# Helping a depthwise convolution: one multiplication and one adding transfer per tap, on wide tiles, and more taps

## The chip, the cores and the metric

The kernel runs on one core of one Trainium2 chip. The metric is the device time of one execution in microseconds (us). The core's engines appear as PE (TensorE, matmuls), PEld (its weight loads), DVE (VectorE), ACT (ScalarE), POOL (GpSimd) and SP (SyncE). GpSimd and SyncE issue the DMA transfers that matter here: GpSimd's go through queue q0, SyncE's through q1, and both are served by the same 16 DMA engines.

## The reference

Eight images of 384 channels and 32 x 32 places, all in f32, pass through two blocks:

```python
# block 0: attention and MLP, over the 1024 places of an image as tokens
h = layernorm(t, g1, beta1)                        # over the 384 channels
q, k, v = split(h @ w_qkv.T + b_qkv)               # 8 heads of 48
t = t + (softmax(q @ k.T * 48**-0.5) @ v) @ w_proj.T + b_proj
h = layernorm(t, g2, beta2)
t = t + gelu_tanh(h @ w_fc1.T + b_fc1) @ w_fc2.T + b_fc2     # 1536 hidden
# block 1: depthwise convolution, MLP with a global response normalization
y = depthwise_conv_7x7(x, dw_w, padding=3) + dw_b  # each channel by its own 49 taps
y = layernorm(y, ln_w, ln_b)
y = gelu(y @ w1 + b1)                              # 1536 hidden
nx = norm_over_places(y) / (mean_over_channels(norm_over_places(y)) + 1e-6)
x = x + (grn_gamma * (y * nx) + grn_beta + y) @ w2 + b2
```

## The kernel before

**Layout.** An image lies in SBUF with its channels on partitions: 3 channel tiles (`ct`, 0 to 2) of 128 partitions by N = 1024 places. `half(h)` is one of the two halves of 512 places. `pad` holds the same image with a border of three places for the convolution, and `acc` the sums of the convolution, [128, 3, 1024]. A matmul of TensorE takes 128 x 512 places at a time.

**Order of the work.** Block 1 of image b-1 runs between the parts of block 0 of image b. One image b (the loop is `for b in range(B)` near the end of the kernel) goes through these stages: the products for q and k (`qk`); attention (64 steps, one head and one block of 128 keys in each: scores at L818, exponential at L827, product with v two steps later at L838); the MLP (`mlp`); the first product of block 1 of image b-1 (`grn_up`); v of the next image (`values`, from `next_values`); the second product of block 1 (`grn_down`), for which y is scaled at L1473. Most products are done by fast schemes with fewer products (15 for 3 x 3 by 2 x 2 blocks) whose operands are sums of blocks; L480 is the evacuation of such a sum or product on ScalarE, L496 and L467 are matmuls of it.

**The flow.** The order of the instructions on each engine is fixed when the program is built. TensorE's main path is written out; with each matmul, `flow.pe(us)` moves a virtual time on (`U` = 0.857 us for 128 x 512). Everything else is a chain (a Python generator) that yields the time it wants to wait; when the virtual time has passed it, the chain records its next instructions. A `paced` chain counts from the time it was due.

**The convolution.** A tap is one of the 49 weights of the 7 x 7 window. VectorE takes most taps: `convolution` (L1244), one instruction a tap and channel tile, `acc = window * weight + acc`. The rest are the helped taps. `help_convolution` takes the last `HELPED[ct]` taps of the list `TAPS` for each channel tile, tile 2 first, then 1, then 0: ScalarE multiplies a window of `pad` by the weight into a tile `tap` (L1279), and GpSimd issues a DMA transfer that adds this tile to `acc` (L1280). A helped tap is done in two halves of 512 places, one instruction and one transfer of 256 KB each, 2.5 us of virtual time apart. The last eight taps of the list are, in order, 48, 23, 3, 10, 17, 31, 38, 45; so HELPED = 5, 7, 7 helps 10 to 45 of channel tile 0 and 23 to 45 of tiles 1 and 2.

`start_conv` spawns both chains for image b behind `grn_up` of image b-1; they run on beside v, the second product of block 1, and q, k and attention of the next image. `taken[ct]` keeps VectorE off the channel tile that is being helped, until 8 us of virtual time after its last helped tap. While the list `quiet` has an entry (during `grn_down`), the helper waits. Images 0 to 6 have helped taps; image 7's convolution runs otherwise.

**Tiles named "res".** The products of helped taps lie in tiles of the tag "res": four buffers of [128, 512] in the pool `three`. A tile that takes a buffer again waits until the last use of this buffer is done, here until the transfer of four halves ago has landed. Three other places use the tag: the loads of the residual in the last product (`grn_down_straight`), a spare of the preparation in image 0 (`spare`), and the four tiles of the first layernorm of the next image (`places` in `norm_of_next`).

**Layernorm.** It sums squares over the 384 channels: VectorE adds the three channel tiles (`ln_sq`), and TensorE sums over partitions with a matmul by ones. `token_sums` first folds `ln_sq`, with `fold="columns"` by two DMA transfers of GpSimd that add one half of the partitions to the other (L526), and then sums with matmuls (L532, `ln_var`) over 64 partitions. The second layernorm of block 0 does this in the second half of attention, where its chain stands beside the helped taps.

Of the kernel before, what the change touches and what calls it, by code (L numbers as in the profile page):

```python
# [46 lines left out]
F32 = mybir.dt.float32  # L47
AF = mybir.ActivationFunctionType
ALU = mybir.AluOpType
AX = mybir.AxisListType  # L50

P = 128
B, C, H, W = 8, 384, 32, 32
N = H * W
# [5 lines left out]
KS, PAD = 7, 3  # L60
HP, WP = H + 2 * PAD, W + 2 * PAD
NH = N // 2
# [2 lines left out]
CM = 2  # L65
NC = HT // CM
U = 0.857
HELPED = 5, 7, 7
BEGUN = 5
SCALE = HD ** -0.5  # L70
EPS0, EPS1, GRN_EPS = 1e-5, 1e-6, 1e-6
# [105 lines left out]
def block_kernel(  # L177
# [16 lines left out]
    nc = tc.nc  # L194
# [4 lines left out]
    two = ctx.enter_context(tc.tile_pool(name="two", bufs=2))  # L199
# [30 lines left out]
    def half(h):  # L230
        return slice(h * NH, (h + 1) * NH)
# [36 lines left out]
    def col(name, i):  # L268
        at, width = VEC[name]
        assert i < width  # L270
        return vec[:, at + i : at + i + 1]
# [4 lines left out]
    def image(ap):  # L276
        return ap.rearrange("p (h w) -> p h w", w=W)

    def o_tile(name):
        return ps_o.tile([P, NH], F32, tag="o", name=name)  # L280

    def s_tile(name):
        return ps_s.tile([P, N], F32, tag="s", name=name)
# [979 lines left out]
    def help_convolution(acc, us, taken):  # L1263

        yield 8.0
        for ct in reversed(range(CT)):
            taken[ct] = float("inf")
            for i in TAPS[KS * KS - HELPED[ct] :]:
                dy, dx = divmod(i, KS)
                for h in range(2):  # L1270
                    if quiet:
                        while quiet:
                            yield 1.0
                        yield 3.0
                    t = three.tile([P, NH], F32, tag="res", bufs=4, name=f"tap_{ct}_{i}_{h}")
                    y0 = dy + h * H // 2
                    window = pad[:, ct, y0 : y0 + H // 2, dx : dx + W]
                    tap = col("dww", ct * KS * KS + i)
                    nc.scalar.mul(t.rearrange("p (h w) -> p h w", w=W), window, tap)  # L1279
                    nc.gpsimd.dma_start(out=acc[:, ct, half(h)], in_=t, accum_op=ALU.add)  # L1280
                    yield us
            taken[ct] = flow.now + 8.0
        yield 8.0
        taken.clear()
# [73 lines left out]
    def grn_down_straight(b, y, kept, weights, tag, index, todo):  # L1358


        rows = [r for r, _ in todo]
        res = []

        def load():
            if len(res) < len(todo):
                r, part = todo[len(res)]
                t = three.tile([P, NH], F32, tag="res", bufs=4, name=f"res_{b}_{r}_{part.start}")[:, : part.stop - part.start]
                nc.sync.dma_start(out=t, in_=kept[r * P : (r + 1) * P, part])
                res.append(t)

        for _ in range(3):
            load()
        for n, (r, part) in enumerate(todo):
            keys = RAW[2 * r : 2 * r + 2]
            tiles = [weights.at(f"w2_{tag}", key)[:, k, :] for key in keys for k in range(HT // 2)]
            ps = o_tile(f"o2_{b}_{r}")[:, : part.stop - part.start]
            for k in range(HT):
                nc.tensor.matmul(out=ps, lhsT=tiles[k], rhs=y(k, part), start=(k == 0), stop=(k == HT - 1))  # L1378
                flow.pe(U * (part.stop - part.start) / NH)
                if k == 2 and rows.index(r) == n and r + 1 in rows:  # L1380
                    for key in RAW[2 * r + 2 : 2 * r + 4]:
                        scaled(b, weights.at(f"w2_{tag}", key), key, True)
            if r not in rows[n + 1 :]:
                for key in keys:
                    weights.used(f"w2_{tag}", key)
            nc.vector.scalar_tensor_tensor(res[n], ps, b2[:, r : r + 1], res[n], ALU.add, ALU.add)
            nc.sync.dma_start(out=image_of(out, index)[r * P : (r + 1) * P, part], in_=res[n])
            load()
# [253 lines left out]
    def prepare(weights, aside):  # L1642
# [19 lines left out]
            return parts  # L1662

        def spare(name):
            return three.tile([P, NH], F32, tag="res", bufs=4, name=name)

        def forms(name, w, store):
            def keep_form(i, t):
# [198 lines left out]
    def main():  # L1867
# [55 lines left out]
        def start_conv(b, us, *first):  # L1923
            acc = state["acc"] = one.tile([P, CT, N], F32, tag="acc", name=f"acc_{b}")
            taken = {}
            state["conv"] = flow.spawn(convolution(acc, us, first, taken=taken, helped=HELPED, begun=state.pop("begun", {})), paced=True)
            state["help"] = flow.spawn(help_convolution(acc, 2.5, taken), paced=True)

        def conv_norm(b, ln):

# [44 lines left out]
        def norm_of_next(b, us):  # L1975

            xn, name = state["xn"], f"ln1_{b + 1}"
            gates["ln1"] = 0
            places = [three.tile([P, NH], F32, tag="res", bufs=4, name=f"{name}_{i}") for i in range(4)]
            pairs = [(h, places[2 * h], places[2 * h + 1]) for h in range(2)]  # L1980
            quarters = [slice(j * NH // 2, (j + 1) * NH // 2) for j in range(2)]

            def fold(t, h):
                nc.gpsimd.dma_start(out=t[ROWS[h], :], in_=t[ROWS[1 - h], :], accum_op=ALU.add)

            def strip(h, j):
                return slice(64 * h + 32 * j, 64 * h + 32 * j + 32)

            def fold_again(t, h):
                for j, q in enumerate(quarters):  # L1990
                    nc.gpsimd.dma_start(out=t[strip(h, j), q], in_=t[strip(h, 1 - j), q], accum_op=ALU.add)

            def totals(kind, of):

                both_banks = s_tile(f"{name}_{kind}0").rearrange("p (j n) -> p j n", j=2)[:, :, : NH // 2]
                single = [o_tile(f"{name}_{kind}1_{j}")[:, : NH // 2] for j in range(2)]
                for h in range(2):
                    for j, q in enumerate(quarters):
                        out = single[j] if h else both_banks[:, j, :]
                        rows = strip(h, j)  # L2000
                        nc.tensor.matmul(out=out, lhsT=ones[rows, :], rhs=of[h][rows, q], start=True, stop=True)
                flow.pe(U / 2)
                whole = lambda t: t.rearrange("p (j n) -> p j n", j=2)
                return [[(both_banks, whole)], [(single[j], lambda t, q=q: t[:, q]) for j, q in enumerate(quarters)]]

            for h, a, _ in pairs:
                nc.vector.tensor_tensor(a, xn[:, 0, half(h)], xn[:, 1, half(h)], ALU.add)
            for h, a, _ in pairs:
                nc.vector.tensor_tensor(a, a, xn[:, 2, half(h)], ALU.add)
                fold(a, h)  # L2010
            yield 8.0
            for h, a, _ in pairs:
                fold_again(a, h)
            yield us - 8.0
            sums = totals("sum", [a for _, a, _ in pairs])
            yield 0.8
            for h, a, square in pairs:
                for ct in range(CT):
                    part = xn[:, ct, half(h)]
                    for ps, view in sums[h]:  # L2020
                        nc.vector.scalar_tensor_tensor(view(part), ps, -1.0 / C, view(part), ALU.mult, ALU.add)
                    if ct < 2:
                        nc.scalar.activation((square, a)[ct], part, AF.Square)
                yield 3.0
            for h, a, square in pairs:
                nc.vector.tensor_tensor(square, square, a, ALU.add)
                nc.scalar.activation(a, xn[:, 2, half(h)], AF.Square)
                yield 1.5
            for h, a, square in pairs:
                nc.vector.tensor_tensor(square, square, a, ALU.add)  # L2030
                fold(square, h)
            yield 5.0
            for h, _, square in pairs:
                fold_again(square, h)
            yield 8.0
            sums = totals("var", [square for _, _, square in pairs])
            yield 0.8
            ln_table()
            for h, a, _ in pairs:
                for ps, view in sums[h]:  # L2040
                    nc.scalar.activation(view(a), ps, AF.Ln, bias=eps0, scale=1.0 / C)
                nc.scalar.activation(a, a, AF.Exp, scale=-0.5)
            for h, a, _ in pairs:
                for ct in range(CT):
                    yield from gated("ln1")
                    part = xn[:, ct, half(h)]
                    nc.vector.scalar_tensor_tensor(part, part, col("g1", ct), a, ALU.mult, ALU.mult)
# [257 lines left out]
```

## Time and profile before

| | |
|---|---|
| time, median of 3 runs | 3212.09 us (3211.55 to 3214.67) |
| profiled execution, its own time | 3213.02 us |
| its span | 3211.1 us, 39348 instructions |
| mean granted clock of TensorE | 0.999 |
| PE busy | 3196.2 us (100%), 14204 matmuls |
| DVE busy | 2550.4 us (79%), 3587 instructions |
| ACT busy | 1674.6 us (52%), 2363 instructions |
| POOL busy | 493.4 us (15%), 592 instructions |
| DMA | 393.09 MB, mean 122 GB/s; q0 26.6% and q1 23.6% of the 16 engines' span |
| L1244, DVE, taps of the convolution, 815 of one group of shapes | 911.0 us, 1157 ns each |
| L827, ACT, exponentials 128x1024, 512 | 524.3 us, 1025 ns each |
| L1279, ACT, helped taps 128x512, 266 | 195.1 us, 736 ns each |
| L1280, POOL, issues of adding transfers, 266 | 227.0 us, 859 ns each |
| adding transfers acc<-tap, 256.0 KB | 3.5 us median from issue to landing |

Busy times are those of one profiled execution; matmuls are pipelined and their ends are modelled, so a busy PE can still have waited. A row of the page names line, engine, operation and the tiles out<-in, then the count, the busy time and the mean of one, then the idle time of the engine just before these instructions and what ended most of it. An arrow such as "<-DMA acc<-tap" names what released the instruction.

### The profile page before, as it was taken

To read this page: it belongs to the slowest core of one execution; us is meant where nothing else is said; L and a number is where in the kernel's file an instruction comes from. 1 tells how busy PE (TensorE), PEld (TensorE's weight loads), DVE (VectorE), ACT (ScalarE), POOL (GpSimd) and SP (SyncE) were. 2 spreads that over 40 slices of the span, in tenths; PEclk is the share of its full clock that TensorE was granted. 3 is DMA by queue.
4 is the path that set the end of the run, shared out by engine and by line. 5 is a ranking of instruction groups with operands and counts; after the bars stand their busy time and mean duration, and the time that the engine had idled before them with its cause. 6 is when DMAs were issued, how large, how long until landed. Compare 5 with 4: busy or idle time off the path is not lost.

```text
span 3211.1 us, 39348 instructions
## 1 busy us (share of the span) xinstructions
PE 3196.2 (100%) x14204; PEld 1402.1 (44%) x14204; DVE 2550.4 (79%) x3587; ACT 1674.6 (52%) x2363; POOL 493.4 (15%) x592
## 2 busy tenths in 40 slices
PE   9999999999999999999999999999999999999999
PEld 5344434443444434444344443444435444344454
DVE  4547788897878978789787888888887788879964
ACT  3542763456644476444754637637365374732543
POOL 2102211112111121201112011120111201200000
PEclk9999999999999999999999999999999999999999
DMA  6435742647346564456546374463743638433244
GB/s 210 155 127 170 168 90 50 162 112 165 84 88 159 123 151 92 97 142 158 115 92 124 116 186 97 81 136 106 194 92 80 148 97 200 72 81 93 55 119 111
DMA packets 206052, 393.09 MB, mean 122 GB/s; under 512 B 42656, under 2 KB 48416, under 8 KB 205472
## 3 DMA queue, kind: packets, MB, share of 16 engines
q0 software_dynamic: 79296, 163.35, 26.6%
q1 hardware_dynamic: 126272, 226.49, 23.6%
q8 instruction: 114, 1.87, 0.2%
q10 hardware_dynamic: 288, 0.71, 0.1%
q14 instruction: 82, 0.67, 0.1%
HBM read 212.98 MB, written 40.11 MB: 79 GB/s over the span
## 4 chain that ended last, share of the span: by engine, by line
PE 97%; DVE 1%; DMA 1%; ACT 0%; issue 0%; SPq 0%; DVEq 0%; ACTq 0%
PE fc L415 15%; PE s L818 13%; PE o L838 13%; PE o_p L496 11%; PE fc_p L496 11%; PE v L738 4%; PE proj L760 4%; PE h_n L467 3%; PE h_z L467 3%; PE h_x L467 3%; PE h_last L1427 2%; PE o L1378 2%; PE h L402 2%; PE qk_n L467 2%; PE qk_z L467 2%; PE qk_x L467 1%
## 5 line engine op out<-in xcount | busy, mean ns | idle before, releaser
L1244 DVE SCALAR_TENSOR_TENSOR acc<-pad,vec,acc 128x870 f32<-128x870 f32 (+8 forms) x815 | 911.0, 1157 | 2.7
L827 ACT ACTIVATE p<-s 128x1024 f32<-128x1024 f32 x512 | 524.3, 1025 | 255.2 <-PE s L818 246.9
L818 PE MATMUL s<-qk 48*64 48x512 f32 x4096 | 538.7, 591 | 0.4 <-ACT qk L660 0.2
L838 PE MATMUL o<-p,v 64*64 64x512 f32 x4096 | 535.7, 589 | 0.0
L1280 POOL DMA_DIRECT2D acc<-tap x266 | 227.0, 859 | 1354.9 <-ACT tap L1279 647.5
L415 PE MATMUL fc<-xn,fc 128*128 128x512 f32 x972 | 427.7, 594 | 0.1
L496 PE MATMUL o_p<-y,w 128*128 128x512 f32 x664 | 289.0, 592 | 0.0
L838 PEld LDWEIGHTS o<-p,v 64*64 64x64 f32 x4096 | 166.4, 132 | 273.3 <-issue 265.0
L415 PEld LDWEIGHTS fc<-xn,fc 128*128 128x128 f32 x972 | 183.1, 190 | 229.2 <-issue 220.5
L818 PEld LDWEIGHTS s<-qk 48*64 48x64 f32 x4096 | 162.3, 132 | 275.9 <-issue 213.1
L496 PE MATMUL fc_p<-qk,fc 128*128 128x512 f32 x520 | 226.6, 593 | 0.3 <-DMA qk<-qk 0.3
L1279 ACT ACTIVATE tap<-pad,vec 128x512 f32<-128x512 f32 x266 | 195.1, 736 | 2.9 <-DMA acc<-tap 2.9
L496 PEld LDWEIGHTS o_p<-y,w 128*128 128x128 f32 x664 | 125.6, 190 | 157.7 <-issue 146.4
L1244 DVE SCALAR_TENSOR_TENSOR acc_last<-pad,vec,acc_last 128x377 f32<-128x377 f32 (+24 forms) x288 | 177.2, 688 | 0.6
L496 PEld LDWEIGHTS fc_p<-qk,fc 128*128 128x128 f32 x520 | 98.2, 190 | 126.9 <-issue 117.4
L508 ACT ACTIVATE qk<-fc,bfc_f 128x512 f32<-128x512 f32 x90 | 61.6, 685 | 160.4 <-PE fc L415 160.4
L508 ACT ACTIVATE hid<-fc,bfc_f 128x512 f32<-128x512 f32 x72 | 49.4, 687 | 158.3 <-PE fc L415 158.3
L779 DVE TENSOR_TENSOR attn<-o,attn 128x512 f32<-128x512 f32 x64 | 44.1, 689 | 109.9 <-ACT attn L777 108.8
L760 PE MATMUL proj<-attn,wproj_sb 128*128 128x512 f32 x288 | 127.5, 596 | 0.7 <-DVE attn L805 0.7
L738 PE MATMUL v<-wv_sb,xn 128*128 128x384 f32 x384 | 126.8, 487 | 0.0
L991 ACT COPY pad<-x 128x512 f32<-128x512 f32 x42 | 26.3, 634 | 187.7 <-DVE x L1083 187.7
L738 PEld LDWEIGHTS v<-wv_sb,xn 128*128 128x128 f32 x384 | 72.5, 190 | 50.1 <-issue 3.4
(446 smaller groups left out, 4594.7 us busy)
## 6 DMA issues: line engine op xcount, KB each, us to landing
acc<-tap POOLq DMA_DIRECT2D x266, 256.0 KB, 3.5
fc<-s_fc SPq DMA_DIRECT2D x91, 256.0 KB, 3.0
w<-s_w SPq DMA_DIRECT2D x91, 256.0 KB, 2.7
w<-s_w SPq DMA_DIRECT2D x72, 320.0 KB, 4.2
fc<-in_wfc SPq DMA_DIRECT2D x54, 384.0 KB, 4.0
y<-y POOLq DMA_DIRECT2D x38, 512.0 KB, 6.7
qk<-qk POOLq DMA_DIRECT2D x30, 512.0 KB, 9.4
qk<-s_qk SPq DMA_DIRECT2D x42, 320.0 KB, 4.9
```

The lines of the kernel that those rows point to most:

```text
L415: nc.tensor.matmul(out=ps, lhsT=lhsT(k), rhs=rhs(k)[:, half(h)], start=(k == 0), stop=(k == nk - 1))
L467: nc.tensor.matmul(out=at, lhsT=weights.at(wname, g, slot // 5)[:, slot % 5, :], rhs=rhs[n], start=first, stop=True, skip_group_check=not ...
L496: nc.tensor.matmul(out=bank, lhsT=lhsT, rhs=rhs, start=k == 0, stop=k == len(pairs) - 1)
L508: nc.scalar.activation(dst, src, function, **kw)
L738: nc.tensor.matmul(out=ps[:, :C], lhsT=xn[:, k, t * P : (t + 1) * P], rhs=wv_sb[:, k, :], start=(k == 0), stop=(k == CT - 1),)
L760: nc.tensor.matmul(out=ps, lhsT=wproj_sb[:, m, ct * P : (ct + 1) * P], rhs=attn[:, m, :], start=(m == 0), stop=(m == CT - 1),)
L818: nc.tensor.matmul(out=s[64 * i : 64 * i + 64, j, :], lhsT=kT[64 * j : 64 * j + HD, m, k0 : k0 + 64], rhs=qT[64 * j : 64 * j + HD, m, half ...
L827: nc.scalar.activation(p, s, AF.Exp)
L838: nc.tensor.matmul(out=outs[i][64 * j : 64 * j + 64, :], lhsT=v[keys, t, at : at + 64], rhs=p[keys, j, :], start=(t == 0), stop=(t == KT - 1),
L1244: nc.vector.scalar_tensor_tensor(dst, window, tap, dst, ALU.mult, ALU.add)
L1279: nc.scalar.mul(t.rearrange("p (h w) -> p h w", w=W), window, tap)
L1280: nc.gpsimd.dma_start(out=acc[:, ct, half(h)], in_=t, accum_op=ALU.add)
```

## The change

A helped tap is done whole. ScalarE multiplies the window of all 1024 places by one instruction into a tile [128, 1024], and GpSimd adds it to `acc` by one transfer of 512 KB. The tiles of the tag "res" are now two buffers of [128, 1024] in the pool `two`, as much SBUF as the four of [128, 512]; `wide_tile` takes one. The other three places that use the tag get halves of such a tile from `res_tile`. The helper's pace goes from 2.5 us for a half to 4.5 us for a tap. `HELPED` goes from 5, 7, 7 to 6, 8, 8: tap 3 of channel tile 0 and tap 48 of tiles 1 and 2 go from VectorE to the helper. Helped taps go from 19 to 22 an image, their multiplications and transfers from 38 to 22 an image.

```diff
-HELPED = 5, 7, 7
+HELPED = 6, 8, 8
@@ block_kernel
+    wide = []
+
+    def wide_tile(name):
+        wide.clear()
+        return two.tile([P, N], F32, tag="res", name=name)
+
+    def res_tile(name):
+
+        if not wide:
+            t = wide_tile(name)
+            wide.extend((t[:, half(1)], t[:, half(0)]))
+        return wide.pop()
@@ help_convolution
             for i in TAPS[KS * KS - HELPED[ct] :]:
                 dy, dx = divmod(i, KS)
-                for h in range(2):
-                    if quiet:
-                        while quiet:
-                            yield 1.0
-                        yield 3.0
-                    t = three.tile([P, NH], F32, tag="res", bufs=4, name=f"tap_{ct}_{i}_{h}")
-                    y0 = dy + h * H // 2
-                    window = pad[:, ct, y0 : y0 + H // 2, dx : dx + W]
-                    tap = col("dww", ct * KS * KS + i)
-                    nc.scalar.mul(t.rearrange("p (h w) -> p h w", w=W), window, tap)
-                    nc.gpsimd.dma_start(out=acc[:, ct, half(h)], in_=t, accum_op=ALU.add)
-                    yield us
+                if quiet:
+                    while quiet:
+                        yield 1.0
+                    yield 3.0
+                t = wide_tile(f"tap_{ct}_{i}")
+                nc.scalar.mul(image(t), pad[:, ct, dy : dy + H, dx : dx + W], col("dww", ct * KS * KS + i))
+                nc.gpsimd.dma_start(out=acc[:, ct, :], in_=t, accum_op=ALU.add)
+                yield us
             taken[ct] = flow.now + 8.0
@@ grn_down_straight
-                t = three.tile([P, NH], F32, tag="res", bufs=4, name=f"res_{b}_{r}_{part.start}")[:, : part.stop - part.start]
+                t = res_tile(f"res_{b}_{r}_{part.start}")[:, : part.stop - part.start]
@@ prepare
         def spare(name):
-            return three.tile([P, NH], F32, tag="res", bufs=4, name=name)
+            return res_tile(name)
@@ start_conv
-            state["help"] = flow.spawn(help_convolution(acc, 2.5, taken), paced=True)
+            state["help"] = flow.spawn(help_convolution(acc, 4.5, taken), paced=True)
@@ norm_of_next
-            places = [three.tile([P, NH], F32, tag="res", bufs=4, name=f"{name}_{i}") for i in range(4)]
+            places = [res_tile(f"{name}_{i}") for i in range(4)]
```

## The prediction

> **What bounds the kernel now.** I read the page first, for the shares and the chain, then the waits of TensorE between 400 and 2830 us (images 1 to 6 and the start of 7), then the timelines of the places where taps stand next to work that TensorE waits for.
>
> ```profile
> PE 3196.2 (100%) x14204; PEld 1402.1 (44%) x14204; DVE 2550.4 (79%) x3587; ACT 1674.6 (52%) x2363; POOL 493.4 (15%) x592
> ...
> PE 97%; DVE 1%; DMA 1%; ACT 0%; issue 0%; SPq 0%; DVEq 0%; ACTq 0%
> ...
> L1280 POOL DMA_DIRECT2D acc<-tap x266 | 227.0, 859 | 1354.9 <-ACT tap L1279 647.5
> ...
> L1279 ACT ACTIVATE tap<-pad,vec 128x512 f32<-128x512 f32 x266 | 195.1, 736 | 2.9 <-DMA acc<-tap 2.9
> ```
>
> TensorE is the bound, and the helped taps stand on three engines that are not. A busy TensorE can hide waits, since ends are modelled, so I went by starts: a pass of 512 columns follows the last one after 429 ns. Starts later than that sum to about 40 us over the run, 18 of them in image 0, before the first tap; images 1 to 7 have about 3 us each, nearly all in fixed gaps of about 0.1 us that recur in every image where one kind of matmul follows another. What an engine or a transfer makes TensorE wait for there is this:
>
> ```profile
> PE ln_var L532 <- DVE acc L1244: 0.7, 1, 0.7
> PE fc_p L496 <- DMA qk<-qk: 0.3, 1, 0.3
> ```
>
> With some smaller late starts I count 2.5 us that could be gained in the part that the change touches. The change can therefore hardly win; the question is what it makes late.
>
> **The change part by part.** *VectorE* loses three taps an image, 21 in all: 21 x 1.157 us (the row of L1244) = 24 us. TensorE waited 0.7 us for VectorE there: worth 0, at most the 2.5 us above. Its cover is a VectorE that is idle a fifth of the time. *ScalarE* makes 154 multiplications of 128x1024 instead of 266 of 128x512 (736 ns). The new one lies between 1.03 us (the exponential of the same size) and two halves, 1.47; I take 1.2, near the scaling of y from SBUF at 1.14. In attention one exponential (1.02 us) is due every 1.72 us and may end up to 1.55 us late, because its score bank is needed again 2.57 us after the scores; a tap of 1.2 and the copy of an average (0.58) before one exponential make it 0.8 late. Worth 0. *GpSimd* issues 154 transfers instead of 266, about 0.86 us each, on a queue with 1354.9 us of idle time before them: 0. *Bytes added* go from 266 x 256 KB to 154 x 512 KB, 68 to 79 MB, at a DMA share of one half: 0 by themselves. The order on TensorE and SyncE's loads stay as they are; the spare tiles of the preparation in image 0 keep their places in time and only share wide buffers.
>
> *Two wide buffers* pay at one place: tap n+2 waits on ScalarE for the landing of tap n, with the evacuations of the k product behind it. And each transfer into one channel tile waits on GpSimd for the landing of the one before it, since both add to the same bytes; until now two halves went side by side. Image 3:
>
> ```profile
> 1138.92 0.74 ACT L1279 ACTIVATE tap<-pad,vec 128x512 f32<-128x512 f32 x1 [0.69 <-DMA acc<-tap]
> 1139.77 0.60 ACT L480 ACTIVATE qk<-qk_x 128x512 f32<-128x512 f32 x1
> ```
>
> With four half buffers this tap already waits 0.69 us. The L480 behind it starts when its product is ready, at 1139.77, and the TensorE product at 1141.29 needs it: 0.85 us to spare. In the changed order the whole fourth tap of the stage stands here and waits for the second, which goes out at about 1131.6. Its two halves went out at 1130.1 and 1131.2, got their first bytes at 1135, when the loads before them had drained, and landed at 1138.8 and 1141.6. Bounds for the whole: 1138 (served in one stretch) to 1141.6 (like the halves), so a TensorE stall of 0 to 1.9 us in six images, 0 to 11. I take 0: fewer, longer pieces need fewer turns against the other queue. In image 1, where the chain of landings starts later, the same sum gives 0.7 to 2; I take 1.0.
>
> *The fold of the second layernorm* is where I expect the loss. In the second half of attention GpSimd issues a tap and right behind it two transfers that add the halves of ln_sq, which TensorE needs for ln_var:
>
> ```profile
> 1243.36 0.78 ACT L1279 ACTIVATE tap<-pad,vec 128x512 f32<-128x512 f32 x1
> ...
> 1244.43 0.83 POOL L1280 DMA_DIRECT2D acc<-tap  x1 [1.19 <-ACT tap L1279]
> 1244.97 2.02 POOL L526 DMA_DIRECT2D ln_sq<-ln_sq  x2
> ...
> 1249.20 0.61 PE L532 MATMUL ln_var<-ln_sq,ones 64*64 64x256 f32 x8
> ...
> DMA to landing us min/median/max: 3.4/3.4/3.4
> ```
>
> Issued at 1244.97 and 1245.51, the folds land 3.36 later, the second at 1248.87: 0.33 before TensorE needs it. Over images 1 to 7 this spare is 0.32, 0.00, 0.33, 0.01, 0.17, -0.22 and -0.01 us. In the changed order the whole tap 17 stands right before these folds in images 2 to 7, and the sum of ScalarE's rows puts its end where the half's was (two separate halves before it become one whole). So the folds go out at the same time, behind twice the bytes. In the trace's packets an adding piece of 1, 2 and 3 KB takes 113, 184 and 252 ns; I estimate 320 for 4 KB. Eight to a DMA engine: 2.56 us against 1.47, so the folds land 1.07 later. Bounds: 0 (a piece costs the same at twice the size) and 1.8 (512 KB adding transfers in 2 KB pieces land after 5.0 at best, taps after 3.2). Image by image 1.07 less the spare: 1.07, 0.74, 1.06, 0.90, 1.07, 1.07 (no more than the delay where the spare was negative). In image 1 the fold stands behind tap 31, whose later end costs another 0.45: 1.2. Sum 7.1 us, all on the path, for the attention's score products are queued behind ln_var on TensorE.
>
> The Trainium skill (DMA: Bandwidth & Descriptors, "Anatomy of one DMA") puts a GpSimd transfer at 2.0 us plus bytes at 436 GB/s: a tap would grow by only 0.6 us, and the stalls would be an estimated 3.8 us instead of 7.1. The taps here grow in the adding itself, by 70 ns a KB and engine, so I stay with the rows. The same page ("Two DMAs through the same engine are not ordered") says that descriptors of one queue start in order, which speaks against longer transfers ahead of a fold.
>
> *Scaling of y* before the last matmul stage: the eighth scaled slice ends 0.13 us before TensorE takes it, and two whole taps before it take 0.1 to 0.2 more of ScalarE than three halves: 0 to 0.1 an image; I take 0.3 in all.
>
> **Sum.** 7.1 + 1.0 + 0.3 = 8.4 us. The profiled execution took 3213.0 (span 3211.1 and 1.9 around it), so 3221.4; the median of the runs lies 0.9 lower: 3220.5.
>
> **Rivals.** (1) *Not slower*: the price of an adding piece goes with the piece, not its bytes. The place is the queue ahead of the ln_sq folds; it decides at about 290 ns for 4 KB: below that the seven stalls stay under 5.4 us and the whole within 6.4. At 184 the folds land as before and the time is 3212 to 3214. For it: copies of 4 KB on the same queue take 162 ns. Against it: the even growth over three sizes of adding pieces. (2) *The buffer wait decides*: the second tap of the q/k stage lands as late as its halves, ScalarE stops, and six images lose 1.9 each on top: 3232. For it: the 0.69 us wait with twice the buffers. Against it: in one stretch it lands three microseconds sooner. (3) *Faster through the relief* of VectorE, ScalarE and GpSimd: bounded by 2.5 us, 3209.6; only image 0's waits could add more, and no tap runs there. (4) *The change doesn't do what it says*: the wide transfer goes out as two pieces of 2 KB a row. Then it grows by 1.47 instead of 1.07, and 7 x 0.4 more gives 3223; this lies inside the forecast.
>
> **How the numbers follow.** A measurement of this kernel tells about 0.2%, 6.4 us, from no change. Folds late, with or without (4): 0.45. Buffer wait on top: 0.17. Both are slower. Not slower: 0.34. Faster by more than 6.4 us: 0.04, since that needs more than the 2.5 us that I found. The time is that of the likeliest case, 3220.5. The range runs from 3211.5 (folds hidden, a little gained) to 3234 (buffer wait at its full price and some of the 1.8 bound).
>
> **What would show it.** Right: ln_var L532 becomes the largest wait of TensorE, about 1 us once in each of seven images, on the fold's transfer; ln_sq folds land 4.4 us after issue instead of 3.4; taps of 512 KB land after 4.3 at best. Rival 2: a wait of tap on acc<-tap of over 2 us just before L480, with late qk_x starts. Rival 1: taps land after 3.3 and the waits of TensorE stay as short as they are. Wrong altogether: a loss outside the q/k stage and the second half of attention, or waits of exponentials on taps all through attention.

## The result, and the profile after

The changed kernel takes 3264.89 us (median of 4 runs, 3260.79 to 3269.36) against 3212.3 before, beside it: a ratio of 1.0165 (1.0153 to 1.0177). The forecast was 3220.5, its range ended at 3234.0. The direction was right and the size wrong by a factor of six. The profiled execution took 3269.36, with a span of 3267.5: 56.4 more than the span before. In the changed kernel L831 is the score product, L840 the exponential, L1288 and L1289 the multiplication and the transfer of a tap, L493 and L501 evacuations on ScalarE, L539 and L545 the fold and its sum.

The page of the changed kernel: busy times, the chain that ended last, and the groups that answer to those of before.

```profile
PE 3216.6 (98%) x14204; PEld 1401.6 (43%) x14204; DVE 2532.3 (77%) x3566; ACT 1667.5 (51%) x2251; POOL 398.9 (12%) x480
...
PE 77%; DMA 7%; ACT 3%; issue 1%; DVE 1%; SPq 0%; POOL 0%; ACTq 0%; DVEq 0%; POOLq 0%
...
L1288 ACT ACTIVATE tap<-pad,vec 128x1024 f32<-128x1024 f32 x154 | 182.0, 1182 | 51.7 <-DMA acc<-tap 51.6
```

Every engine beside TensorE is less busy than before, and the kernel is slower. The chain left TensorE: DMA went from 1% to 7%, ScalarE from 0 to 3%. A multiplication costs 1182 ns, as the sum had it (1.2 us). What is new is the 51.6 us that ScalarE stood in front of these instructions until a transfer had landed and a buffer was free; before it was 2.9.

The waits of TensorE, images 1 to 7 (total us, times, longest):

```profile
PE ln_var L545 <- DMA ln_sq<-ln_sq: 11.8, 8, 2.4
PE qk_x L480 <- ACT qk L493: 11.7, 6, 2.9
PE s L831 <- ACT p L840: 10.6, 10, 1.9
PE qk_n L480 <- ACT qk L501: 1.6, 1, 1.6
```

Three places, not one: the folds, the q/k stage (with image 1 in the last line), and the exponentials of attention. The waits sum to 36.8 us with three small ones. The timelines of image 3 show where they start. ScalarE in the q/k stage, at the fourth tap of the stage:

```profile
1159.54 1.19 ACT L1288 ACTIVATE tap<-pad,vec 128x1024 f32<-128x1024 f32 x1 [4.65 <-DMA acc<-tap]
1160.63 0.58 ACT L493 ACTIVATE qk<-qk_x 128x512 f32<-128x512 f32 x1
```

The tap waits 4.65 us for the buffer of the second tap, whose transfer landed 9.3 us after its issue. The evacuation of a product, L493, stands behind it in ScalarE's fixed order, and TensorE waits 2.89 us for it. GpSimd, in the first half of attention:

```profile
1200.08 0.85 POOL L1289 DMA_DIRECT2D acc<-tap  x1 [4.22 <-ACT attn L790]
1205.42 0.84 POOL L1289 DMA_DIRECT2D acc<-tap  x1 [4.50 <-DMA acc<-tap]
1211.02 0.85 POOL L1289 DMA_DIRECT2D acc<-tap  x1 [4.75 <-DMA acc<-tap]
```

The transfers go out 5.3 and 5.6 us apart, each after the landing of the one before it, since both add to the same bytes. A whole tap lands 4.46 us after its issue at best, and the next is issued 0.53 after that: 5.0 us a tap, with loads beside it more. The helper asks for one every 4.5. ScalarE in the same stretch:

```profile
1204.91 1.20 ACT L1288 ACTIVATE tap<-pad,vec 128x1024 f32<-128x1024 f32 x1 [0.47 <-DMA acc<-tap]
1206.02 1.91 ACT L840 ACTIVATE p<-s 128x1024 f32<-128x1024 f32 x2
1210.51 1.19 ACT L1288 ACTIVATE tap<-pad,vec 128x1024 f32<-128x1024 f32 x1 [2.58 <-DMA acc<-tap]
```

Transfers go out later and later behind their multiplications, until ScalarE stands still for a buffer, 0.47 us and then 2.58, with the exponentials behind it; TensorE waits 1.63 us for a score bank at 1212.66.

The fold of image 3, on GpSimd; before, it went out at 1244.97, 0.54 after an unhindered tap:

```profile
1263.82 0.83 POOL L1289 DMA_DIRECT2D acc<-tap  x1 [4.22 <-ACT p L840]
1269.47 0.84 POOL L1289 DMA_DIRECT2D acc<-tap  x1 [4.82 <-DMA acc<-tap]
1270.01 2.01 POOL L539 DMA_DIRECT2D ln_sq<-ln_sq  x2
```

VectorE's last sum for it ended at 1267.74; the fold left 2.3 us later (0.3 before the change), since it stood behind a tap that itself waited for a landing. Then it landed 5.2 us after issue instead of 3.4.

The granted clock, in two stretches of image 3 (columns: start and end, length, busy time of the engines, then PEclk, DMA share, GB/s):

```profile
1162.50:1165.50 3.00, 3.00 (x4) 1.00 (x3) 0.69 (x1) 1.18 (x2) 0.00 (x0) 0.50 0.75 137
1275.00:1282.00 7.00, 6.62 (x36) 4.04 (x40) 3.92 (x7) 3.38 (x5) 1.73 (x2) 0.51 0.49 106
```

TensorE had stood still up to 1161.3 (q/k stage) and up to 1275.4 (fold). Around these two points the clock fell to one half, for 3.4 and 6.8 us. From 300 us to the last matmul the record of the clock has seven such stretches, 27.3 us in all; half of that, 13.7, is my estimate of what they cost. Before the change it has none. So of the 56.4 us, 36.8 are waits, some 13.7 are the low clock behind them, and some 6 are spread in pieces that I did not trace.

### The profile page after: what moved, and what is told of

The parts are those of the page before. It is cut to its first block, busy times and chain, and to the rows that moved or that the text cites. A ratio compares the mean times of both kernels' runs of the same rounds, so it can differ in the third digit from the quotient of the medians.

```text
span 3267.5 us, 38987 instructions
## 1 busy us (share of the span) xinstructions
PE 3216.6 (98%) x14204; PEld 1401.6 (43%) x14204; DVE 2532.3 (77%) x3566; ACT 1667.5 (51%) x2251; POOL 398.9 (12%) x480
## 4 chain that ended last, share of the span: by engine, by line
PE 77%; DMA 7%; ACT 3%; issue 1%; DVE 1%; SPq 0%; POOL 0%; ACTq 0%; DVEq 0%; POOLq 0%
PE fc L428 12%; PE o_p L509 11%; PE fc_p L509 10%; PE s L831 9%; PE o L851 8%; DMA acc<-tap 5%; PE h_n L480 3%; PE v L751 3%; PE proj L773 3%; PE h_x L480 3%; PE h_z L480 3%; PE h_last L1436 2%; PE o L1387 2%; PE h L415 2%; ACT p L840 1%; PE h_k L480 1%
## 5 line engine op out<-in xcount | busy, mean ns | idle before, releaser
L1257 DVE SCALAR_TENSOR_TENSOR acc<-pad,vec,acc 128x899 f32<-128x899 f32 (+7 forms) x794 | 890.8, 1159 | 3.6 <-DVE inv L799 0.2
L840 ACT ACTIVATE p<-s 128x1024 f32<-128x1024 f32 x512 | 521.4, 1022 | 268.8 <-PE s L831 268.3
L831 PE MATMUL s<-qk 48*64 48x512 f32 x4096 | 561.6, 595 | 10.9 <-ACT p L840 10.8
L851 PE MATMUL o<-p,v 64*64 64x512 f32 x4096 | 557.4, 592 | 0.0
L1289 POOL DMA_DIRECT2D acc<-tap x154 | 131.1, 851 | 1352.9 <-DVE gscale L1464 502.5
L831 PEld LDWEIGHTS s<-qk 48*64 48x64 f32 x4096 | 165.6, 133 | 294.1 <-issue 244.4
L1288 ACT ACTIVATE tap<-pad,vec 128x1024 f32<-128x1024 f32 x154 | 182.0, 1182 | 51.7 <-DMA acc<-tap 51.6
```

Source lines behind the costliest of these rows:

```text
L831: nc.tensor.matmul(out=s[64 * i : 64 * i + 64, j, :], lhsT=kT[64 * j : 64 * j + HD, m, k0 : k0 + 64], rhs=qT[64 * j : 64 * j + HD, m, half ...
L840: nc.scalar.activation(p, s, AF.Exp)
L851: nc.tensor.matmul(out=outs[i][64 * j : 64 * j + 64, :], lhsT=v[keys, t, at : at + 64], rhs=p[keys, j, :], start=(t == 0), stop=(t == KT - 1),
L1257: nc.vector.scalar_tensor_tensor(dst, window, tap, dst, ALU.mult, ALU.add)
L1288: nc.scalar.mul(image(t), pad[:, ct, dy : dy + H, dx : dx + W], col("dww", ct * KS * KS + i))
L1289: nc.gpsimd.dma_start(out=acc[:, ct, :], in_=t, accum_op=ALU.add)
```

## The experiments

Theory *Queue*: whole transfers into the same bytes are a chain that needs 5.0 us a tap, and the pace asks for one every 4.5. It holds for attention; the q/k stage turns out to have a cause of its own (see *The pace* and *The q/k stage by itself*). In this table "whole" is one transfer of 512 KB from one of two wide buffers, "halves" two of 256 KB from four; the times of before beside the runs lie between 3211.6 and 3212.3.

| helped taps | form | pace, us a tap | time, us | ratio to before |
|---|---|---|---|---|
| 5, 7, 7 | halves | 5.0 (before) | 3212 | 1 |
| 5, 7, 7 | halves | 4.5 | 3216.27 | 1.0014 (1.0004 to 1.0023) |
| 5, 7, 7 | whole | 6.0 | 3217.91 | 1.0019 (1.0009 to 1.0028) |
| 5, 7, 7 | whole | 5.0 | 3236.94 | 1.0077 (1.0060 to 1.0094) |
| 5, 7, 7 | whole | 4.5 | 3273.95 | 1.0194 (1.0177 to 1.0211) |
| 6, 8, 8 | halves | 5.0 | 3216.11 | 1.0013 (1.0003 to 1.0022) |
| 6, 8, 8 | whole | 5.2 | 3215.69 | 1.0012 (1.0002 to 1.0022) |
| 6, 8, 8 | whole | 5.0 | 3227.78 | 1.0043 (1.0029 to 1.0058) |
| 6, 8, 8 | whole | 4.5 (the change) | 3264.89 | 1.0165 (1.0153 to 1.0177) |

**Which part of the change: the form alone, more taps alone.**

```diff
 e1_only_wide, in the changed kernel
-HELPED = 6, 8, 8
+HELPED = 5, 7, 7
 e2_only_more, in the kernel before
-HELPED = 5, 7, 7
+HELPED = 6, 8, 8
```

> Wide tiles and whole transfers alone: HELPED is 5, 7, 7 as before, the pace 4.5 us a tap. Theory Queue: a whole tap's transfer takes 4.5 us at best and the next one into the same channel tile is issued 0.5 us after its landing, so the chain needs 5.0 us a tap at least and is asked for one every 4.5; GpSimd's queue falls behind, the folds of ln_sq stand in it, and ScalarE stops for buffers. The rate is the same here, so most of the loss stays: 3240 to 3262, waits on folds, on qk in the q/k stage and on exponentials all there. Rival More taps: the three more taps an image overload ScalarE and the queue; then this is 3212 to 3222 with TensorE's waits below 5 us.

> More taps alone: HELPED 6, 8, 8 in halves on four buffers, the pace 2.5 us a half. Theory Queue: a half lands after 3.3 us and the next one into the same half comes 5 us later, so nothing falls behind: 3210 to 3218, TensorE's waits as before. Rival More taps: most of the loss is here, 3240 or more.

e1 took 3273.95 us, above the 3262 that I gave as its end, with all three waits (14.0 on folds, 12.4 in the q/k stage, 9.6 on exponentials); e2 took 3216.11. So the three taps more are not the cause. They cost 4 us in halves, by a wait I had not foreseen: `ln_sum` on VectorE's `ln_a`, 4.8 us in five images, where late taps of the convolution stand ahead of it. With whole transfers six, eight and eight taps are 9 us *better* than five, seven and seven, at 4.5 and at 5.0 alike. Part of it is where the folds fall among the taps (waits on folds 14.0 against 11.8, and 12.6 against 7.1 at 5.0); the rest is open.

**The pace.** Whole transfers at 6.0 us; and the whole change at 5.2 and at 5.0, the old rate.

```diff
-            state["help"] = flow.spawn(help_convolution(acc, 4.5, taken), paced=True)
+            state["help"] = flow.spawn(help_convolution(acc, 6.0, taken), paced=True)   # e3, with HELPED = 5, 7, 7
+            state["help"] = flow.spawn(help_convolution(acc, 5.2, taken), paced=True)   # e7, HELPED = 6, 8, 8
+            state["help"] = flow.spawn(help_convolution(acc, 5.0, taken), paced=True)   # e10, HELPED = 6, 8, 8; e11, 5, 7, 7
```

> Wide tiles and whole transfers, HELPED 5, 7, 7, the pace 6.0 us a tap instead of 4.5: longer than the 5.0 us that the chain needs. Theory Queue: in attention GpSimd no longer waits for landings, the waits of TensorE on exponentials go (below 1 us in all), the folds come out 1 us late at most (below 7 us in all), what stays is the q/k stage, where loads of SyncE hold up the taps' landings: 8 to 14 us with its low clock. In all 3222 to 3238. Rival Longer multiplication: ScalarE's 1.18 us in one piece makes the exponentials late whatever the pace; then their waits stay at 7 us or more. Rival Longer transfer: the folds stay at 1.4 us or more each, since it is the transfer ahead of them that holds them and not the queue.

> The whole change with a pace of 5.2 us a tap instead of 4.5, all else the same. Theory Queue: just above the 5.0 us of the undisturbed chain and below the 5.4 that issues lie apart in the changed kernel; the queue still grows, but slowly: waits on exponentials 0 to 4, on folds 4 to 9, q/k stage 6 to 12: 3225 to 3245. Rival More taps: with the three taps more the stalls stay what they are, 3255 or more.

> The whole change at the rate of before: 5.0 us a tap, as two halves of 2.5 us were. HELPED 6, 8, 8, whole transfers, two wide buffers. Theory Queue: this is the point at which the chain, 5.0 us at best and more beside loads, just fails to keep up: between the 3216 of 5.2 and the 3265 of 4.5, nearer to the first: 3218 to 3235. Rival Form alone: the wide form costs most of its loss at the old rate too, 3250 or more.

> The wide form alone at the rate of before: HELPED 5, 7, 7, whole transfers, two wide buffers, 5.0 us a tap; against the kernel before only the form differs. Theory Queue: as with 6, 8, 8 at 5.0, 3218 to 3235, between 3218 at 6.0 and 3274 at 4.5. Rival Form alone: 3250 or more.

e3 took 3217.91, better than I gave it: the q/k stage lost nothing either. e7 took 3215.69, again better: going from 4.5 to 5.2 us a tap was worth 49 of the 53 us. e10 and e11 took 3227.78 and 3236.94, the first inside the range of Queue, the second 2 us above it. The largest wait of TensorE and the one of ScalarE for buffers in e7, the whole change at 5.2, images 1 to 7 (TensorE's others sum to 1.2):

```profile
PE ln_var L545 <- DMA ln_sq<-ln_sq: 1.0, 1, 1.0
...
ACT tap L1288 <- DMA acc<-tap: 0.9, 1, 0.9
```

The same whole transfers, the same two buffers, the same 1.18 us on ScalarE: the waits are gone. The rivals Longer multiplication and More taps fall here. At 5.0 (e10) the waits on folds are 7.1 us in all, those on exponentials none. That the loss bends up between 5.2 and 4.5 has two parts. Below the chain's own 5.0 a backlog adds up. And the pace moves taps in ScalarE's fixed order, which I had overlooked. In e7 the fourth tap of the q/k stage of image 3 stands behind the evacuation, not ahead of it:

```profile
1143.40 0.60 ACT L493 ACTIVATE qk<-qk_x 128x512 f32<-128x512 f32 x1 [0.72 <-PE qk_x L480]
...
1153.32 1.19 ACT L1288 ACTIVATE tap<-pad,vec 128x1024 f32<-128x1024 f32 x1
```

The second tap's transfer took as long here (9.5 us to landing, 9.3 in the changed kernel); only the instruction that needs its buffer comes some 12 us later in the stage. In images 1 to 7 of the changed kernel, e1, e4 and e5 (all at 4.5) that tap stands ahead of the stage's last L493, and TensorE waits there in six images, 9.6 to 15.7 us in all. In those of the other runs with wide tiles (e3, e6, e7, e8, e10, e11) it stands behind, and TensorE waits there in image 1 at most.

e3 also shows the price of a whole tap ahead of a fold without any queue. In image 1 the fold stands right behind a tap that left on time (GpSimd's timeline):

```profile
463.56 0.84 POOL L1289 DMA_DIRECT2D acc<-tap  x1 [4.45 <-ACT tap L1288]
464.29 1.81 POOL L539 DMA_DIRECT2D ln_sq<-ln_sq  x2
```

The two transfers of `ln_sq` landed 4.9 and 5.1 us after issue, 1.5 to 1.7 later than the 3.4 behind a half in image 3, but only 0.7 and 1.0 later than those of image 1 before the change (4.25 and 4.08), and TensorE waited 0.6 us. In images 2 to 7 the fold left ahead of the tap and TensorE did not wait, so e3 tests the rival Longer transfer by one image only. Images 3 to 5 of e6 (below) add three: the fold left 0.2 to 0.3 us later than before the change, behind a whole tap, its transfers landed 1.0 to 1.4 later after issue than those of the same image before the change, and TensorE waited 0 to 0.25. In image 7 of e7 the fold left 0.7 later and TensorE waited 1.0. So a whole tap ahead of a fold can cost, but not the 1.7 an image that the folds cost in the changed kernel.

**The transfer: in halves, out of the wide tile.** In the whole change (e4, pace 4.5), and with 5, 7, 7 at 6.0 (e8).

```diff
-                nc.gpsimd.dma_start(out=acc[:, ct, :], in_=t, accum_op=ALU.add)
+                for h in range(2):
+                    nc.gpsimd.dma_start(out=acc[:, ct, half(h)], in_=t[:, half(h)], accum_op=ALU.add)
```

> The whole change but for one thing: each wide tile is added to acc by two transfers of 256 KB, one for each half, instead of one of 512 KB. HELPED 6, 8, 8 and the pace 4.5 stay, and ScalarE's multiplication stays whole. Theory Queue: two chains of landings side by side, each needs 3.3 + 0.5 us a tap, less than 4.5: waits on exponentials gone, folds as before the change within 0.5 us each, some of the q/k stage's buffer wait left: 3212 to 3226. Rival Two buffers: they are too few whatever the transfer, ScalarE's waits for buffers stay above 25 us and the time above 3240. Rival Longer multiplication: exponentials late by 7 us or more in all.

> The wide multiplication alone: HELPED 5, 7, 7, one multiplication a tap into a wide tile, two transfers of 256 KB, pace 6.0. Theory Queue: nothing is left to fall behind; 3210 to 3216, as before the change, and the relief of ScalarE is worth nothing. If the 6 us by which whole transfers at this pace are slower than before come from the whole transfer, they go here; if they come from the later end of the helped taps, they stay (3216 to 3220).

The two largest waits of TensorE in e4:

```profile
PE qk_x L480 <- ACT qk L493: 15.7, 6, 3.3
PE ln_var L545 <- DMA ln_sq<-ln_sq: 7.5, 6, 1.8
```

e4 took 3252.66, 1.0127 (1.0111 to 1.0144), where I had said 3226 at most. Queue was right for attention: two chains side by side keep up, and the exponentials wait 0.4 instead of 10.6. It was wrong for the rest. The q/k stage got worse (15.7), so there the rival Two buffers holds at this pace: ScalarE still stood 32.3 us for buffers, and 40 of the 53 us stay. And the folds still wait 7.5, behind two transfers that went out when ScalarE had multiplied their tap. e8 took 3218.36, 1.0021 (1.0011 to 1.0030), with 2.7 us of waits. At 6.0 no difference between whole transfers and halves shows, so the 6 us by which e3 stands above before are not the transfer's.

**The same bytes.** Channel tiles 2 and 1 helped in turn.

```diff
-        for ct in reversed(range(CT)):
-            taken[ct] = float("inf")
-            for i in TAPS[KS * KS - HELPED[ct] :]:
+        helped = [TAPS[KS * KS - HELPED[ct] :] for ct in range(CT)]
+        both = [(ct, i) for pair in zip(helped[2], helped[1]) for ct, i in zip((2, 1), pair)]
+        for group in (both, [(0, i) for i in helped[0]]):
+            for ct in {ct for ct, _ in group}:
+                taken[ct] = float("inf")
+            for ct, i in group:
...
-            taken[ct] = flow.now + 8.0
+            for ct in {ct for ct, _ in group}:
+                taken[ct] = flow.now + 8.0
```

> The whole change (6, 8, 8, pace 4.5, whole transfers, two wide buffers), but channel tiles 2 and 1 are helped in turn, tap by tap, so that two transfers in a row never add to the same bytes. VectorE is kept off both tiles for that time and does its missing taps late, ahead of the norm behind the convolution; so the time itself (3350 to 3500) says nothing here, and only the waits of attention are read. Theory Queue: what a transfer waits for is the landing of the one before it in the same bytes; with tiles in turn GpSimd issues each one without that wait while both tiles last, and TensorE's waits on exponentials go below 2 us in all (10.6 in the changed kernel); the folds of images 2 to 7, which stand among the taps of channel tile 0, wait 1 us or so each. Rival Capacity: the DMA engines themselves cannot add 512 KB every 4.5 us beside the loads; then landings grow to 8 us and more in attention and the exponentials' waits stay near 10.

GpSimd in the first half of attention, image 3:

```profile
1237.15 0.84 POOL L1292 DMA_DIRECT2D acc<-tap  x1 [3.83 <-ACT tap L1291]
1242.31 0.85 POOL L1292 DMA_DIRECT2D acc<-tap  x1 [4.32 <-ACT tap L1291]
1246.54 0.84 POOL L1292 DMA_DIRECT2D acc<-tap  x1 [3.38 <-ACT tap L1291]
```

Now each transfer goes out when its tap is ready, 5.2 and 4.2 us apart here, 3.4 at the least up to 1256 us; the waits on exponentials are 0.4 us in all. The transfers land after 5.1 us in the median from 1200 to 1256 us, not after 8, so Capacity falls; it is the landing in the same bytes that GpSimd waited for. The folds wait 10.6 us, 1.8 each, and not the 1 that I expected: among the taps of channel tile 0 the chain is what it was. The q/k stage waits 9.6. The time, 3459.6, is that of VectorE's late taps.

**The q/k stage by itself.** A wait of 6.0 us after each of the first four taps of an image, 4.5 after the rest. Two of the four run beside v, ahead of `grn_down`, and two in the q/k stage, so the expectation below names them wrongly.

```diff
-            for i in TAPS[KS * KS - HELPED[ct] :]:
+            for n, i in enumerate(TAPS[KS * KS - HELPED[ct] :]):
...
-                yield us
+                yield 6.0 if ct == 2 and n < 4 else us
```

> The whole change, but the first four taps of each image, those of the q/k stage, come 6.0 us apart instead of 4.5. Theory Queue: the buffer wait of the q/k stage is a matter of its own, set by SyncE's loads ahead of the landings and by the pace there; the waits on qk fall from 11.7 to below 3 us in all, while the waits on exponentials (about 10) and on folds (about 12) stay, since the pace there is still below the 5.0 us of the chain: 3240 to 3255. Rival One cause: the queue of the q/k stage is what attention inherits, and without it the other waits go as well: 3225 or less.

The largest waits of TensorE in e6:

```profile
PE ln_var L545 <- DMA ln_sq<-ln_sq: 3.6, 3, 2.4
PE s L831 <- ACT p L840: 2.5, 6, 0.6
```

3229.25, 1.0051 (1.0034 to 1.0067), between the two theories and outside both ranges. The waits of the q/k stage are gone, as expected; but those on exponentials went from 10.6 to 2.5 and those on folds from 11.8 to 3.6. So most of the loss on exponentials and folds is inherited from the q/k stage; later taps shift by up to 6 us as well in e6, which I can't separate. In image 3 of the changed kernel the fourth tap of the stage went out 5.3 us after it was multiplied, in e6 0.3 us after. What starts the backlog is the load on the other queue, seen in the DMA answer for 1149.2 to 1154.2 us of the changed kernel; the second tap of the stage was issued at 1150.2:

```profile
q1 hardware_dynamic: 878, 1.84, 101.7%
q0 software_dynamic: 1, 0.00, 0.0%
...
acc<-tap POOLq DMA_DIRECT2D x1, 512.0 KB, 9.3
```

SyncE's loads took all 16 engines for five microseconds, the tap's queue got one packet, and it landed 9.3 us after its issue. Halves before the change met the same: those of this tap landed 8.7 and 10.4 us after issue. So the late landing is not new. New is that at 4.5 a whole tap ahead of an evacuation needs all of that buffer back; at 5.0 or more the tap stands behind the evacuation.

**The pace alone, in the old form.**

```diff
-            state["help"] = flow.spawn(help_convolution(acc, 2.5, taken), paced=True)
+            state["help"] = flow.spawn(help_convolution(acc, 2.25, taken), paced=True)
```

> The kernel before with one number changed: the pace of its halves is 2.25 us instead of 2.5, which makes a tap every 4.5 us as in the changed kernel, in halves, on four buffers, HELPED 5, 7, 7. Theory Queue: a half's chain needs 3.3 + 0.5 us and is asked for one every 4.5, so attention keeps up: no waits on exponentials, folds below 3 us in all; the q/k stage alone is short of buffers there, by 0 to 2 us a time: 3212 to 3226. Rival Pace alone: it is the faster pace and not the whole transfer that does it; then the three kinds of waits come up here as well, 3240 or more.

3216.27, with TensorE's waits at 2.7 us in all: Pace alone falls. It takes the wide tiles *and* the pace of 4.5. Taken away alone, the whole transfer is worth 12 us of the loss (e4), the fourth tap's place in the q/k stage with what follows from it some 36 (e6). What stays open is a remainder of 4 to 6 us that all variants with small waits have against the kernel before (e3, e7, e8, e9), of which the waits name 2 to 3. No variant is faster than the kernel before.

## Why the prediction was wrong, step by step

- *GpSimd, "on a queue with 1354.9 us of idle time before them: 0".* This is one of two steps that failed, the other is the buffer wait below. Idle time over the run says nothing of a chain with a rate. The prediction did say that transfers into one channel tile wait for each other's landing and that two halves went side by side until now, but used it at one place only. The sum that was missing is one line: 4.3 us, the landing I forecast for 512 KB myself, plus half a microsecond, against a pace of 4.5. What the runs showed: 5.0 us a tap, and waits on exponentials of 10.6 us that fall to 0.4 when transfers in a row have other bytes (e4, e5).
- *The pace.* The diff takes it from 5.0 us a tap to 4.5. I did not weigh this line at all; with the form it is 37 us of the 53 (3227.78 at 5.0 against 3264.89), in part because it decides on which side of an evacuation a tap stands.
- *"Two wide buffers pay at one place".* This step failed most. They paid at three: 28 waits of ScalarE, 51.6 us. The place in the q/k stage was right, the fourth tap ahead of the evacuation, but of bounds 0 to 1.9 I took 0; measured were 1.4 to 3.1 late per image, 11.7 in six. "Fewer, longer pieces" did not help: the whole second tap landed 9.3 us after issue, between its halves of before (8.7 and 10.4). The upper bound was too low as well, since it took the second tap's issue from the old timeline, while the landing before it moved that issue, too. And nothing was set down for what follows: with the wait gone the time is 3229.25 (e6).
- *ScalarE in attention, "worth 0".* The multiplication's length was right (1.18 against 1.2) and costs nothing, as e7 shows. What made exponentials late was the wait for a buffer in front of it.
- *The folds, 7.1 us.* Right place, wrong working: the waits were 11.8; that those of e10, at 5.0, sum to 7.1 is chance. "The folds go out at the same time" was false, they left 0.3 to 2.0 us later behind waiting taps. The spare was misread, too: the first passes of ln_var need only the first of the two transfers (in image 4 after the change the passes start at 1675.30 and 1676.37, the landings are at 1675.17 and 1676.33), so most spares were about 0.2 us longer than I had them; and the delay by the longer transfer, 1.07 in the sum, was near: 0.7 to 1.4 image by image where the fold left almost on time (e3, e6). What the sum lacked is the later issue. A 4 KB adding piece measured 336 ns (estimate 320), so rows beat rival 1 (decision at 290). By the Trainium skill's price for a transfer (DMA: Bandwidth & Descriptors, "Anatomy of one DMA") a tap of twice the size takes an estimated 0.6 us more; measured were 1.24 (3.22 to 4.46 at best), and the measurement decides.
- *Rival 2, the buffer wait.* The mechanism that started most of the loss was given 0.17 and 3232 us. Its price in the q/k stage, six times 1.9, was near the measured 11.7; the low clock and what follows into attention were missing.
- *The clock.* No term of the sum had it: some 13.7 us of the profiled execution, more than the forecast loss.

## What to carry to other kernels

Before two transfers are merged into one of twice the size, write down the rate of the chain they form: landing plus the next issue, times the number of transfers that must follow each other in the same bytes, against the pace at which they are asked for. The idle time of the issuing engine over the run does not answer that, and a queue that falls behind by half a microsecond a turn shows up far away: at whoever shares the queue, and at whoever needs the buffer. Then look at what stands behind the instruction that needs the buffer back: here a change of pace by half a microsecond moved it from ahead of an evacuation that TensorE needs to behind it, and most of the loss went with it. Where TensorE is the bound, price a stall above its length, since the clock can fall behind it.

## What the hardware showed that I had not expected

**A short stall can halve the clock behind it.** I took all starts of TensorE that came over 1 us late, from 300 us on, in the two kernels and ten experiments (e5 left out). Of the 25 up to 1.75 us late none was followed by a stretch at one half; of 34 between 1.76 and 2.71, 14 were; of the 10 from 2.81 on, all. The stretches last 3.41 us or twice that. The Trainium skill (TensorE: Matmul & The Clock Gate, "HAM oscillation — how this bites in real kernels") gives the rule "no PE-idle gaps >~3.4µs"; here shorter stalls were enough, and the measurement decides. Why, of two stalls of the same length, one is followed by it and the other is not, no run here settles.

**A queue can be shut out for microseconds.** While SyncE's loads kept all engines busy, a GpSimd transfer issued in that time got at most one packet through (above). In the q/k stage of image 3 whole taps landed after 7.3 and 9.3 us, against 4.46 undisturbed; before the change halves landed there after 8.7 and 10.4, against 3.22.

**Adding pieces cost by their bytes.** Median time of one packet of an adding transfer: 111 to 113 ns for 1 KB, 178 to 184 for 2 KB, 252 for 3 KB, 336 for 4 KB, about twice that of plain pieces (84 ns for 2 KB and 161 for 4 KB on SyncE's queue).
